# A masked attention layer on one core: the second batch's third value, token sums and a weight's split change places, and seven more clock-keeping products

## The chip, the cores and the metric

The kernel runs on one core of one Trainium2 chip. The metric is device time in microseconds, from one execution of the whole program. The engines of the core work at the same time and meet at semaphores: PE (matrix products, with PEld for its weight loads), DVE (vector work), ACT (exponentials, copies and scalings), POOL (which issues gathers and scatters by index) and SP (which issues the other transfers). The profile gives the granted clock of PE beside the busy times; 1.00 is full speed.

## The reference

Sixteen batches of x, each 512 features by 1024 tokens, go through one attention layer with eight heads of 64, and the result is added to x. Query, key and value are the same projection. The mask (about half of the 1024 tokens of each batch are on) acts on keys and on queries.

```python
xt = jnp.transpose(x, (0, 2, 1))
q = xt @ Wq.T
qh = q.reshape(B, T, NH, dk).transpose(0, 2, 1, 3)
scores = scale * jnp.einsum('bhqd,bhkd->bhqk', qh, qh)
logits = (scores * cmask + (1.0 - cmask) * NEG) * rmask
attn = jax.nn.softmax(logits, axis=-1)
ctx = jnp.einsum('bhqk,bhkd->bhqd', attn, qh)
out = ctx.transpose(0, 2, 1, 3).reshape(B, T, D) @ Wo.T
return x + jnp.transpose(out, (0, 2, 1))
```

A token whose mask is off gets logits of 0 throughout, so its attention is the plain mean of all tokens' q. Such a token needs no scores of its own: all of a batch's tokens that are off share one row, the projection of the mean of x.

## The kernel before

**Tiling.** The batches are worked through in an order of their number of tokens that are on. Of each batch only those tokens are gathered (up to 544, in blocks of 128 and a tail), by `gather` on POOL. `xt` transposes a block of 128 tokens by PE into a buffer `pm` of PSUM (there are two such buffers, shared by all small products), and `xsplit` takes it out as a high half `xh` (float16, by ACT) and a low half `xl` (by DVE). A query block (`query`, 12 products of float16: high with high, high with low, low with high, over four chunks of 128 features) is copied by ACT and masked by DVE. `qsplit` makes high and low halves of a pair of heads on DVE, and four transfers on SP (`xx<-hl`) lay them out for the scores. `value` brings a pair's queries back into rows of tokens by PE: 8 products with `xx` as weights (L687) for every batch but the first. Its squares are summed on DVE; `peaks`, `top` and `bottom` make of them the shift `nm` that the exponentials subtract.

**The mean.** All 1024 tokens of a batch are loaded by SP in four chunks (`load_all`, 512 KB each, two buffers `xm`), and each chunk is summed over its tokens, by ACT (`sum_half`) or, for batch 1, by DVE (`sum_all`, L535). The sums become one or two extra columns of `xh` and `xl`, filled by the last `xt` of the next batch, so the second half of that batch's first query waits for them.

**Stages.** A batch has 18 stages: four pairs of heads, two rounds of scores each, and a few stages between. `scores` is 16 products of PE, followed by four exponentials on ACT which write p. `attend` multiplies p with the values, one stage after the pair's last exponentials; `tail_scores` does the tail of 32 tokens; `recip_sums` and `recip_rows` make the reciprocals of the sums (a transpose by PE at L958, a transfer `rd` to DRAM and two transfers `rb` back, spread over partitions), and `norm` multiplies them in. While batch b is in its scores, the plan of b puts the queries and values of batch b + 1, and the projection of batch b − 1 with the output weight, between them.

**What sets the order.** PE runs in the order in which the program is written: the dictionary `plan` says which small pieces come in which stage, before or after the stage's attend. The other engines' order is made by a scheduler from priorities and its own costs. `behind(i)` adds an edge: what is written under it comes after instruction `i` on the same engine. `free` lists pieces of the other engines by stage; what runs over the end of a batch goes into `owed` and is taken up by the next one. SP, ACT, DVE and POOL take their instructions strictly in the order they were given.

**Start.** Before the first tokens are there, PE computes the places of the tokens and then `warm` products (128x512, float16, whose result nobody reads, L434): 7, then 12, then 1 and 2 between the first transposes. `split` makes the high part of a weight chunk on ACT (L194) and its `rest` the low part on DVE (L197). For the output weight, `wide_high` and `wide_rest` place these: the high parts in stages 9, 10, 16 and 17 of batch 0, the low parts in stages 0 to 3 of batch 1.

The lines that the prediction speaks of: L268 to L272 slots, L394 index, L434 warm, L528 and L535 token sums, L543 loads, L550 mean columns, L553 and L554 x halves, L595 token transposes, L624 and L628 queries and their copies, L658 to L661 the xx transfers, L684 and L687 values, L691 their copy, L738 and L741 peaks, L747 and L757 top and bottom, L760 nm, L773 corr, L798 and L803 tail scores and their exponential, L855 and L879 scores and exponentials, L904 attend, L958 to L971 recip_rows, L1011 norm.

Of the kernel before, what the change touches and what calls it, by code (L numbers as in the profile page):

```python
# [15 lines left out]
ALU = mybir.AluOpType  # L16
# [9 lines left out]
DC = D // P  # L26
# [21 lines left out]
class Fast:  # L48
# [481 lines left out]
    def sum_all(self, b, c, other):  # L530
        s = self.st[b]
        if not other:
            return self.sum_half(b, c)
        with self.behind(self.last_hl), self.nc.allow_low_precision(reason="float32"):
            self.nc.vector.tensor_reduce(s["ms2"][:, c:c + 1], s["xm"][c], AX.X, ALU.add)  # L535

    def load_all(self, b, c, after=None):
# [195 lines left out]
    def peaks(self, b, g):  # L733

        nc, s = self.nc, self.st[b]
        hs = slice(HG * g, HG * g + HG)
        sm = self.smcol[g][:, :HG]
        nc.vector.tensor_reduce(sm.rearrange("p (e h) -> p e h", h=2),  # L738
                                s["sd"][:, 2 * g:2 * g + 2, :].rearrange("p e (k h) -> p e h k", h=2), AX.X, ALU.max)
        if s["A"] > 512:  # L740
            nc.vector.tensor_tensor(sm, sm, s["sdt"][:, hs], ALU.max)  # L741

    def top(self, b, g):

# [403 lines left out]
    def run(self, flag):  # L1148
        B = self.B
        L = lambda f, *a: lambda: f(*a)  # L1150
# [12 lines left out]
        def value(n, e):  # L1163
            return [(0.45, L(self.value, n, e))]
# [11 lines left out]
        for b in range(2, B):  # L1176
            n = 1 if b < B - 3 else 2 if b == B - 3 else 1 if b == B - 2 else len(queue)
# [38 lines left out]
            self.setup2()  # L1216
        for i in range(DC):
            self.load_half(0, i)
        self.warm(12)
        sums0 = [(0, L(self.sum_half, 0, k)) for k in range(2 * DC)]  # L1220
        for _, f in sums0[:4]:
            f()
# [1 line left out]
        with self.tc.high_priority(offset=HPO):  # L1224
            self.slots_of(1)
        self.setup3()
        self.warm(1)
        self.xt(0, 1)
        self.warm(2)
        self.xt(0, 2)  # L1230
        for i in range(DC, 2 * DC):
            self.load_half(0, i, self.pe)
# [49 lines left out]
        todo, carry, owed = [], [], {}  # L1282
        if True:
            for b in range(B + 1):
                o, n = b - 1, b + 1
# [18 lines left out]
                vt = lambda o, g: [(0.25, L(self.value_tail, o, g))] if self.wide[o] > 512 else []  # L1304
                pk, tp, bt = ((lambda o, g, f=f, c=c: [(c, L(f, o, g))]) for f, c in ((self.peaks, 0), (self.top, 0.1), (self.bottom, 0.1)))
                new = [g for g in groups if b == g[0] - 2], [g for g in groups if b == g[0] - 1]
                turn = [(0.1, L(self.recip_rows, b, p)) for p in (1, 2)]
                if n < B:
                    q, x, v = (lambda e, g: query(n, e, g)), xt(n), (lambda e: [(0.25, L(self.value, n, e))])
                    tc, tv = ((lambda g, f=f, c=c: [(c, L(f, n, g))]) for f, c in ((self.tail_copy, 0), (self.value_tail, 0.25)))  # L1310
                    rng = [(0, L(self.range_x, n, c)) for c in range(DC)]
                    ahead = b + 2 < B
                    hot, index = ([(c, L(f, b + 2))] if ahead else [] for f, c in ((self.hot, 0), (self.index, 0.2)))
                    take = [(0, L(self.gather, b + 2, j)) for j in range(5 if self.wide[b + 2] > 512 else 4)] if ahead else []
                    if self.wide[n] == 512:
                        tc = tv = lambda g: []
                    if b:
                        pre = [(0, L(f, *g)) for g in new[0] for f in (self.permute, self.active)]
                        post = [(0.3, L(self.slots, *g)) for g in new[0]]
                        pre += [(0, L(self.facts_sums, *g)) for g in new[1]]  # L1320
                        end = [(0.1, L(self.facts_end, *g)) for g in new[1]]
                        plan = {(0, 0): sums + x[:2], (0, 1): x[2:4],
                                (3, 0): rows + x[4:] + q(0, 0) + second, (3, 1): pre + q(0, 1) + carry, (4, 0): value(b, 3),
                                (5, 1): vt(b, 1) + pk(b, 1),
                                (7, 0): third + q(1, 0) + tp(b, 1), (7, 1): q(1, 1) + post + end + P_(0) + bt(b, 1), (8, 0): tc(0) + v(0) + rng[:2],
                                (10, 0): tv(0) + tail + q(2, 0), (11, 0): hot + rng[2:] + early,
                                (12, 0): turn[:1] + q(2, 1), (12, 1): index + P_(1) + v(1), (13, 0): take[:3],
                                (14, 1): rest + pk(n, 0), (16, 0): turn[1:] + P_(2) + take[3:], (16, 1): q(3, 0) + tp(n, 0) + q(3, 1),
                                (17, 0): bt(n, 0) + v(2) + tc(1) + [(0, L(self.means, n))]}
                        carry = P_(3)  # L1330
                    else:
                        pre = [(0, L(f, *g)) for g in new[0] for f in (self.permute, self.active)]
                        post = [(0.3, L(self.slots, *g)) for g in new[0]]
                        plan = {(0, 0): query(0, 3, 0) + value(0, 2),
                                (3, 0): query(0, 3, 1) + [(0.1, L(self.facts_end, 0, 2))] + x[:1],
                                (5, 0): value(0, 3) + x[1:2] + pk(b, 1), (5, 1): x[2:4],
                                (7, 0): x[4:] + pre + tp(b, 1) + q(0, 0) + bt(b, 1) + q(0, 1), (8, 1): post + q(1, 0),
                                (11, 0): hot + q(1, 1),
                                (12, 0): tc(0) + v(0) + rng[:2] + q(2, 0), (13, 0): index + q(2, 1) + turn[:1],
                                (14, 0): tv(0) + v(1) + rng[2:] + take[:3], (14, 1): pk(n, 0),  # L1340
                                (16, 0): turn[1:] + q(3, 0) + tp(n, 0) + q(3, 1) + take[3:], (16, 1): bt(n, 0),
                                (17, 0): v(2) + tc(1) + [(0, L(self.means, n))]}
                else:

                    places = [("xi", 8), ("xa", 13)]
                    come = [[L(self.late, x, j, *places[k % 2]) for j in range(5, 9)] for k, x in enumerate(rests[b])]
                    leave = [[L(self.rest, x, j) for j in range(5, 9)] for x in rests[b]]
                    free[0] = come[0]
                    for c, l in zip(come[1:] + [[]], leave):
                        free[0] += c + l  # L1350
                    plan = {(0, 0): sums + [(0, L(self.spread, x)) for x in rests[b]], (1, 1): second, (3, 0): rows + carry + value(b, 3) + pk(b, 1),
                            (7, 0): third + tp(b, 1) + P_(0) + bt(b, 1), (11, 0): P_(1), (13, 0): P_(2), (14, 1): [(0, self.ranges)],
                            (16, 1): P_(3)}
                if b in (1, 2):
                    plan[12, 1] += [(0, L(range_w, " oq"[b], c)) for c in range(DC)]
                if b == 0:
                    for c in range(DC):
                        if c > 1:
                            free.setdefault(3 * c + 2, []).append(lambda c=c: self.load("o", c, None, self.beat))
                        free.setdefault((9, 10, 16, 17)[c], []).append(L(wide_high, c))  # L1360
                if b == 0:
                    free.setdefault(3, []).append(L(self.sources, 2, B))
                if b == 1:
                    free.setdefault(1, []).extend(owed.pop(1))
                    for c in range(DC):
                        free.setdefault(c, []).append(L(wide_rest, c))
                if b + 2 < B:
                    if b + 2 not in self.st:
                        self.start(b + 2)
                for k, x in enumerate([x for x in (b + 2, self.extra.get(b + 2)) if x is not None and x < B]):  # L1370
                    if x > b + 2:
                        self.start(x)
                    elif b + 2 in self.extra.values():
                        continue
                    for c in range(DC):
                        at = 3 * c + k + (0 if b else 6)
                        free.setdefault(at, []).append(L(self.load_all, x, c) if b else lambda x=x, c=c: self.load_all(x, c, self.beat))
                        at += 2 if b + 2 in self.extra else 4
                        (free if at < N else owed).setdefault(at % N + (at >= N), []).append(L(self.sum_all, x, c, b == 0 and x == 1))
                def fill(st, half):  # L1380
                    for _, f in plan.get((st, half), []):
# [2 lines left out]
                for st, (p, i) in enumerate(S):  # L1384
# [17 lines left out]
                    if i == 3:  # L1402
                        todo.append(lambda after=None, b=b, p=p: self.attend(b, p, after))
                        if p < 3:
                            free.setdefault(st + 1, []).append(L(self.recip_sums, b, p))
                            if not p or n == B:
                                free.setdefault(st + 2, []).append(L(self.recip_rows, b, p))
                            if p < 2:
                                free.setdefault(min(st + 8 + (b == 0), N - 1), []).append(L(self.norm, b, p))
# [149 lines left out]
```

## Time and profile before

| | |
|---|---|
| median of three runs | 953.54 us (950.12 to 954.99) |
| profiled execution | 952.53 us |
| its span, first to last instruction | 950.8 us |
| mean granted clock of PE | 0.994 |
| PE busy | 930.2 us, 98% of the span |
| DVE, ACT, POOL busy | 720.2, 644.6, 303.8 us |
| PE busy from 0 to 50 us, clock | 41.55 us, 0.97 |
| PE busy from 50 to 100 us, clock | 45.58 us, 0.93 |
| PE busy from 170 to 880 us, clock | 708.41 us, 1.00 |
| PE busy from 880 to 951 us, clock | 64.91 us, 0.99 |

The busy time of an engine is summed over its instructions; matmuls overlap in the pipeline, so the start of one and the start of the next say more of their cost than the length of one. In a row of the timeline the first number is the start in microseconds from the start of the span, the second how long it took; in brackets stands how long the engine sat idle just before, and what ended that. Batch 0 has its scores from about 28 to 73 us, batch 1 from about 77 us on.

### The profile page before, as it was taken

How to read it: one execution, taken by the hardware profiler on the slowest of the kernel's cores; microseconds unless marked ns; L12 is line 12 of the kernel's file. 1: busy time of each engine (PE TensorE's matmuls, PEld its weight loads, DVE VectorE, ACT ScalarE, POOL GpSimd, SP SyncE). 2: the span in 40 equal slices, each digit the busy share in tenths (PEclk: the TensorE clock that was granted, in tenths of full speed). 3: DMA queues.
4: the chain of work that ended last, by engine and by line, in shares of the span. 5: the costliest groups of instructions: out<-in, count | busy, mean ns of one | idle time of the engine just before them, and what ended most of it. 6: DMA issues, size and time to landing. Idle time of an engine off the chain costs nothing. (4 is left out here: it accounts for less than half of the span.)

```text
span 950.8 us, 22847 instructions
## 1 busy us (share of the span) xinstructions
PE 930.2 (98%) x8125; PEld 584.5 (61%) x8125; DVE 720.2 (76%) x2461; ACT 644.6 (68%) x1669; POOL 303.8 (32%) x311
## 2 busy tenths in 40 slices
PE   7998999999999999999999999999999999999997
PEld 4565666666666666666666666666666666565543
DVE  7797787876877767888677788768777788686564
ACT  4786767667676676776767688666767866655651
POOL 2110022151342414325053340623425034353452
PEclk9998999999999999999999999999999999999999
DMA  5776556666575666766567687645767757555552
GB/s 180 203 225 174 160 161 177 179 200 183 167 218 171 189 192 192 214 177 192 170 194 216 200 244 212 189 140 146 223 182 232 224 154 212 146 167 149 182 178 104
DMA packets 78568, 176.30 MB, mean 185 GB/s; under 512 B 14480, under 2 KB 22416, under 8 KB 78448
## 3 DMA queue, kind: packets, MB, share of 16 engines
q1 hardware_dynamic: 57392, 107.09, 40.3%
q0 software_dynamic: 21056, 67.68, 22.5%
q8 instruction: 66, 1.08, 0.5%
q14 instruction: 54, 0.44, 0.1%
HBM read 91.36 MB, written 33.91 MB: 132 GB/s over the span
## 5 line engine op out<-in xcount | busy, mean ns | idle before, releaser
L879 ACT ACTIVATE p<-pss,nm 128x528 f32<-128x528 f32 (+2 forms) x512 | 353.9, 702 | 89.6 <-PE pss L855 88.7
L904 PE MATMUL pss<-p,v 128*64 128x264 f32 (+2 forms) x2048 | 242.6, 390 | 0.0
L855 PE MATMUL pss<-xx 128*128 128x118 f16 (+17 forms) x1856 | 215.1, 289 | 0.4 <-ACT p L879 0.2
L1098 POOL DMA_INDIRECT y_out<-xa,idx x68 | 80.2, 1180 | 409.5 <-DVE nq L762 120.8
L904 PEld LDWEIGHTS pss<-p,v 128*64 128x64 f32 x2048 | 141.5, 137 | 85.9 <-issue 6.5
L855 PEld LDWEIGHTS <-xx 128*128 128x128 f16 (+1 forms) x1856 | 103.3, 97 | 79.8 <-issue 30.2
L624 PE MATMUL pm<-xh,wqh 128*128 128x264 f16 (+5 forms) x512 | 142.1, 278 | 2.3 <-DVE xh L550 0.9
L624 PE MATMUL pm<-xh,wql 128*128 128x264 f16 (+5 forms) x512 | 141.4, 276 | 0.0
L624 PE MATMUL pm<-xl,wqh 128*128 128x264 f16 (+5 forms) x512 | 141.3, 276 | 0.1
L624 PEld LDWEIGHTS <-wqh 128*128 128x128 f16 x1024 | 98.7, 99 | 25.8 <-issue 5.2
L491 POOL DMA_INDIRECT xa<-x_in,idx x68 | 71.6, 1053 | 116.2 <-DMA y_out<-xa,idx 45.7
L879 ACT ACTIVATION_READ_ACCUMULATOR p<-pss,nm 128x1 f32 x512 | 105.3, 206 | 0.0
L1029 PE MATMUL pm<-woh,cl 128*128 128x512 f16 x240 | 90.9, 379 | 0.0
L1029 PE MATMUL pm<-wol,ch 128*128 128x512 f16 x240 | 90.9, 379 | 0.0
L1029 PE MATMUL pm<-woh,ch 128*128 128x512 f16 x240 | 90.9, 379 | 0.0
L628 ACT ACTIVATE q<-pm 128x264 f32<-128x264 f32 (+5 forms) x128 | 50.8, 397 | 45.7 <-PE pm L624 45.7
L691 ACT COPY v<-pm 128x512 f32<-128x512 f32 x62 | 36.4, 586 | 62.0 <-PE pm L687 62.0
L1098 POOL DMA_INDIRECT y_out<-xi,idx x60 | 65.8, 1097 | 32.9 <-PE pss L798 12.4
L1029 PEld LDWEIGHTS <-ch 128*128 128x128 f16 x480 | 46.2, 100 | 44.3 <-issue 0.8
L491 POOL DMA_INDIRECT xi<-x_in,idx x60 | 59.9, 998 | 21.1 <-issue 16.5
L927 ACT COPY c<-pss 128x528 f32<-128x528 f32 (+2 forms) x64 | 38.2, 597 | 39.2 <-PE pss L922 26.6
L716 DVE TENSOR_TENSOR tmp<-pm,par 128x256 f32<-128x256 f32 x26 | 11.0, 423 | 64.8 <-PE pm L713 64.8
(253 smaller groups left out, 1519.6 us busy)
## 6 DMA issues: line engine op xcount, KB each, us to landing
xm<-x_nat_in SPq DMA_DIRECT2D x60, 512.0 KB
xx<-hl SPq DMA_DIRECT2D x208, 136.0 KB
rb<-rd SPq DMA_DIRECT2D x72, 132.0 KB
xx<-hl SPq DMA_DIRECT2D x48, 128.0 KB
pt<-c SPq DMA_DIRECT2D x36, 132.0 KB
pt<-p SPq DMA_DIRECT2D x36, 132.0 KB
rb<-rd SPq DMA_DIRECT2D x32, 136.0 KB
ub<-ud SPq DMA_DIRECT2D x16, 256.0 KB
```

The costliest lines, as they stand in the source:

```text
L491: dma = self.nc.gpsimd.indirect_dma_start(out=tile[:n], out_offset=None, in_=self.x, in_offset=bass.IndirectOffsetOnAxis(ap=idx, axis=0))
L624: self.beat = nc.tensor.matmul(pq, lhsT=w[:, c, e * P:(e + 1) * P], rhs=xx[:, c, cols], start=(k == 0), stop=(k == 3 * DC - 1)).ins
L628: self.copied = nc.scalar.activation(s["q"][:, e, cols], pq, AF.Copy, scale=1.0 / (SX * SW)).ins
L691: nc.scalar.copy(v, pv)
L716: nc.vector.tensor_tensor(split(v), pv.rearrange("p k (h d) -> p k h d", h=2), self.par.unsqueeze(1).unsqueeze(3).broadcast_to([P, 2, 2, D ...
L855: m = nc.tensor.matmul(flat[:, c0:c1], lhsT=w, rhs=x, start=banks[n] not in banks[:n], stop=banks[n] not in banks[n + 1:])
L879: e = nc.scalar.activation(t, flat[:, at:at + A], AF.Exp, bias=s["nm"][p // 2][:, p % 2 * 2 + k:p % 2 * 2 + k + 1], scale=SCALE, accum_out ...
L904: mm = nc.tensor.matmul(pav[k * DK:(k + 1) * DK, g], lhsT=s["v"][p][:, i, k * DK:(k + 1) * DK], rhs=ps[k, i][:, cols], start=(i == 3), sto ...
L927: self.context_out = nc.scalar.copy(c[:, :A].rearrange("p (g c) -> p g c", g=2), pav).ins
L1029: mm = nc.tensor.matmul(po[:cols.stop - cols.start], lhsT=a[:, e, cols], rhs=w[:, e, wide], start=(e == 0 and k == 0), stop=(e == DC - 1 a ...
L1098: dma = self.nc.gpsimd.indirect_dma_start(out=self.out, out_offset=bass.IndirectOffsetOnAxis(ap=idx, axis=0), in_=x, in_offset=None)
```

## The change

- The third value of batch 1 (heads 4 and 5) leaves the end of batch 0's plan, stage 17, and stands in batch 1's stage 4, ahead of the fourth.
- `recip_rows` of batch 0's first pair leaves stage 6, which it had by `free`, for stage 7, behind the last token transposes and the first query of batch 1.
- The token sums of batch 1 on DVE get one more edge each for the last two chunks: the third comes behind the last `peaks` (`self.peak`), the fourth behind the last x half (`self.last_xs`). The last token sum of batch 2 (on ACT) moves from the end of batch 0 to stage 2 of batch 1.
- The output weight's first two high parts move to stages 6 and 7 of batch 0, their low parts to stages 8 and 9 of batch 0, and the last two low parts to stages 4 and 5 of batch 1.
- Loads and token sums of batch 3 come two stages later.
- The clock-keeping products become 17, 2 and 3 instead of 12, 1 and 2.

```diff
@@ sum_all @@
-        with self.behind(self.last_hl), self.nc.allow_low_precision(reason="float32"):
+        with self.behind(self.last_hl, *([self.peak] if c == 2 else [self.last_xs] if c == 3 else [])), self.nc.allow_low_precision(reason="float32"):
             self.nc.vector.tensor_reduce(s["ms2"][:, c:c + 1], s["xm"][c], AX.X, ALU.add)
@@ peaks @@
         if s["A"] > 512:
-            nc.vector.tensor_tensor(sm, sm, s["sdt"][:, hs], ALU.max)
+            self.peak = nc.vector.tensor_tensor(sm, sm, s["sdt"][:, hs], ALU.max).ins
@@ run @@
-        self.warm(12)
+        self.warm(17)
...
-        self.warm(1)
+        self.warm(2)
         self.xt(0, 1)
-        self.warm(2)
+        self.warm(3)
         self.xt(0, 2)
...
-                turn = [(0.1, L(self.recip_rows, b, p)) for p in (1, 2)]
+                turn = [(0.1, L(self.recip_rows, b, p)) for p in range(3)]
...
-                                (12, 0): turn[:1] + q(2, 1), (12, 1): index + P_(1) + v(1), (13, 0): take[:3],
-                                (14, 1): rest + pk(n, 0), (16, 0): turn[1:] + P_(2) + take[3:], (16, 1): q(3, 0) + tp(n, 0) + q(3, 1),
+                                (12, 0): turn[1:2] + q(2, 1), (12, 1): index + P_(1) + v(1), (13, 0): take[:3],
+                                (14, 1): rest + pk(n, 0), (16, 0): turn[2:] + P_(2) + take[3:], (16, 1): q(3, 0) + tp(n, 0) + q(3, 1),
                                 (17, 0): bt(n, 0) + v(2) + tc(1) + [(0, L(self.means, n))]}
+                        if b == 1:
+                            plan[4, 0] = value(b, 2) + plan[4, 0]
...
-                                (7, 0): x[4:] + pre + tp(b, 1) + q(0, 0) + bt(b, 1) + q(0, 1), (8, 1): post + q(1, 0),
+                                (7, 0): x[4:] + pre + tp(b, 1) + q(0, 0) + bt(b, 1) + q(0, 1) + turn[:1], (8, 1): post + q(1, 0),
...
-                                (16, 0): turn[1:] + q(3, 0) + tp(n, 0) + q(3, 1) + take[3:], (16, 1): bt(n, 0),
-                                (17, 0): v(2) + tc(1) + [(0, L(self.means, n))]}
+                                (16, 0): turn[2:] + q(3, 0) + tp(n, 0) + q(3, 1) + take[3:], (16, 1): bt(n, 0),
+                                (17, 0): tc(1) + [(0, L(self.means, n))]}
...
-                        free.setdefault((9, 10, 16, 17)[c], []).append(L(wide_high, c))
+                        free.setdefault((6, 7, 16, 17)[c], []).append(L(wide_high, c))
+                        if c < 2:
+                            free.setdefault(8 + c, []).append(L(wide_rest, c))
...
                 if b == 1:
-                    free.setdefault(1, []).extend(owed.pop(1))
-                    for c in range(DC):
-                        free.setdefault(c, []).append(L(wide_rest, c))
+                    for k in (1, 2):
+                        free.setdefault(k, []).extend(owed.pop(k))
+                    for c in (2, 3):
+                        free.setdefault(c + 2, []).append(L(wide_rest, c))
...
-                        at = 3 * c + k + (0 if b else 6)
+                        at = 3 * c + k + (0 if b > 1 else 2 if b else 6)
...
-                        at += 2 if b + 2 in self.extra else 4
+                        at += 2 if b + 2 in self.extra and (b or k or c < DC - 1) else 4
...
-                            if not p or n == B:
+                            if n == B or b and not p:
                                 free.setdefault(st + 2, []).append(L(self.recip_rows, b, p))
```

## The prediction

> **What bounds the kernel now.** I read the page first: it says which engine is full.
>
> ```profile
> span 950.8 us, 22847 instructions
> PE 930.2 (98%) x8125; PEld 584.5 (61%) x8125; DVE 720.2 (76%) x2461; ACT 644.6 (68%) x1669; POOL 303.8 (32%) x311
> ```
>
> PE is the bound. An engine that is 98% busy can gain in two ways only: from its few idle microseconds, and from stretches in which it is busy at a lower clock. So the table of windows comes next: PE is busy 708.41 of the 710 us from 170 to 880, and 50 us from 120 to 170 lack 0.28. Nothing is to be had there; the last 71 us lack 6.1, but the change touches nothing in them. What it can move lies before 120 us, where PE lacks 8.5 us in 0 to 50 and 4.4 in 50 to 100, at clocks of 0.97 and 0.93. The windows of 1 and 2 us show where (columns: span, PE, PEld, DVE, ACT, POOL busy, clock, DMA share, GB/s).
>
> ```profile
> 11.00:12.00 1.00, 0.17 (x1) 0.00 (x0) 1.00 (x7) 0.75 (x3) 0.69 (x2) 1.00 0.93 270
> 12.00:13.00 1.00, 0.00 (x0) 0.00 (x0) 0.77 (x4) 0.58 (x2) 0.84 (x1) 1.00 0.71 180
> 14.00:15.00 1.00, 1.00 (x8) 0.60 (x6) 0.96 (x5) 0.47 (x2) 0.10 (x1) 0.83 0.63 213
> 15.00:16.00 1.00, 0.99 (x4) 0.37 (x3) 0.97 (x4) 0.44 (x1) 0.00 (x0) 0.50 0.78 246
> 18.00:19.00 1.00, 1.00 (x11) 0.92 (x9) 0.96 (x8) 0.19 (x1) 0.00 (x0) 0.97 0.84 248
> ...
> 74.00:76.00 2.00, 0.00 (x0) 0.00 (x0) 1.34 (x6) 1.32 (x3) 1.24 (x2) 1.00 1.00 245
> 76.00:78.00 2.00, 0.95 (x10) 0.63 (x11) 1.60 (x9) 0.17 (x1) 0.65 (x1) 0.52 0.94 303
> 78.00:80.00 2.00, 2.00 (x13) 0.97 (x13) 1.14 (x5) 0.83 (x3) 0.00 (x0) 0.50 0.55 212
> 82.00:84.00 2.00, 2.00 (x15) 1.21 (x15) 1.41 (x3) 1.74 (x5) 0.00 (x0) 0.77 0.69 169
> ```
>
> The reader is to see two pairs: PE stands still, and a little later its clock is halved. From the shares, half clock lasts from 14.66 (0.34 of that us) to 18.06, 3.40 us, and from 76.08 to 82.92, 6.84 us, twice as long. Half of that is lost: 1.7 and 3.4 us. The timeline of PE and its waits name what it stood still for:
>
> ```profile
> PE pm L687 <- DMA xx<-hl: 3.2, 2, 2.5
> PE pss L595 <- DMA xa<-x_in,idx: 1.9, 1, 1.9
> ...
> 44.66 0.33 PE L958 MATMUL pm<-ident,rcol 128*128 128x128 f32 x1 [0.98 <-DVE xl L554]
> 76.30 0.21 PE L687 MATMUL pm<-two,xx 128*128 128x64 f16 x1 [2.49 <-DMA xx<-hl]
> 77.26 0.53 PE L687 MATMUL pm<-two,xx 128*128 128x64 f16 x7 [0.75 <-DMA xx<-hl]
> 92.80 0.29 PE L624 MATMUL pm<-xh,wqh 128*128 128x274 f16 x1 [0.94 <-DVE xh L550]
> ```
>
> Idle gaps of 0.94 and 0.98 us kept the clock; 1.87 (11.17 to 13.04) and 3.24 did not. So the third value of batch 1 costs 3.24 of waiting and 3.4 of clock, and the wait for the first gathered tokens, which no order of PE removes, costs 1.7 of clock behind it.
>
> **The change, part by part.** Durations are rows of this execution; the sum is made against its own 952.53 us (span 950.8, 1.7 around it). The median of the runs shown is 953.54.
>
> *Seven more clock-keeping products.* At full clock one costs 0.215 us (twelve in the 2.75 us from 8.42). Five end at 12.25 instead of 11.17, under the wait for the gather (13.04), so they cost nothing and the gap shrinks from 1.87 to 0.8, below the gaps that kept the clock. The other two lie on PE: xt(0,1) moves from 14.14 to 14.36, xt(0,2) from 15.66 to about 15.5, because the three products ahead of it run at full clock. The first query needs the second block's low half (DVE, 15.47 + 0.69 = 16.16), so it starts at 16.2 instead of 16.54, and takes 1.3 us (the same twelve products from 18.61 on at full clock, with the transposes out) instead of 2.07: 17.5 against 18.61. The fourth gather is issued at 13.15 and the first took 3.9, so it is there at 17.05. DVE keeps up, because the built program puts two more query-weight low parts (0.37 each) into DVE's 1.11 us wait before 13.88: its fourth x half comes 1.1 earlier too. Gain 1.1; bounds: 1.7 (all of the lost clock) and a loss of 0.43 (the two products, nothing kept).
>
> *Row sums of pair 0 (recip_rows) moved behind two queries of batch 1.* At 44.66 the transpose waited 0.98 for a pm buffer. Now the scores behind it (44.83) start at 43.7, since their exponentials ended at 41.5. What is late next: pm has two buffers and the moved transpose takes one between the queries, so q(1,1,0) waits for ACT's copy of q(1,0,1), behind a 1.07 sum (49.37): it starts about 0.3 earlier, not 1.1. Its queue matters too: rd and two rb issues now stand directly ahead of the four xx issues of pair 0 on SP, and rb waits for rd, 2.5 us from 45.42 to 47.91. xx then issues about 0.6 later; PE asks for it at 59.6, the trace's packets of this size end at about 57.5, and a 512-KB load is gone from ahead of pair 1's. Gain 0.3; bounds 1.0 and a loss of 0.6. On the facts' product (0.28 wait on DVE eh) DVE's order puts eh ahead of a 0.69 square: gain 0.2.
>
> *Output weight.* Two high parts on ACT (0.52 pitch) move into ACT's 1.23 wait before 42.71: nothing, covered by that wait. Two low parts (0.6 each) enter DVE at 53, where it is full to 72; but the third token sum (1.13 pitch) leaves the same stretch, behind the peaks. The next PE step that needs DVE there, the transpose of the peaks, has 0.7 of slack (71.31 to 72.02). Nothing, bounds 0.3 either way.
>
> *Third value to batch 1's stage 4.* PE ends `bottom` at 73.67, and the exponentials of the last scores ended at 73.19, so the first scores of batch 1 run at 73.7 to 75.4, not 77.60 to 80.64. Both pm buffers are free (copies at 73.5 and, since a 1.07 sum leaves ACT's place between them, 74.3), the first three gathers have landed: transposes to 76.4, attend (3.7) to 80.1. POOL's order is the same: the fourth and fifth gathers are issued at 74.46 and 75.71, and with the first one's 3.9 they are there at 78.4 and 79.6, ahead of their transposes at 81. What is late next is ACT:
>
> ```profile
> 74.72 0.69 DVE L1011 TENSOR_TENSOR c<-c,rb 128x512 f32<-128x512 f32 x1 [0.66 <-DMA rb<-rd]
> 75.33 0.15 DVE L760 TENSOR_SCALAR nm<-pss 128x4 f32<-128x4 f32 x1
> ```
>
> DVE takes the shift nm behind a product that waits for rb. rb is issued 0.5 later now (two xx issues ahead, not one). So nm at about 75.9, corr at 77, and ACT: exponential, two x halves, three exponentials (0.7, 0.5 each) end at 81.2, then the moved token sum (1.2), then the tail's exponential (0.7) to 83.1. The second scores need that one: 83.2 against 87.87. The chain behind it on DVE to the mean columns (L550) was 4.8 us after the tail's exponential; the four weight parts leave it, the last token sum stays in it: about 4.9. So q(2,0,1) starts at 88.1 against 92.80. Gain 4.7, with PE idle about 1.1 and 1.35 on the way. Bounds: 6.6 (both waits and all clock back) and 0 (the wait returns in another place).
>
> *What batch 1 pays later.* Value 2 and 3 now come in a row: value 3 needs the buffer of q(2,0,1), copied 0.4 after it, about 0.2 of wait; and DVE gets two squares (1.3) and two weight parts (1.3) more ahead of peaks(1,1), whose slack was 1.2 (102.92 to 104.15); it also waited 0.5 there. About 0.4. Loads and sums of batch 3 two stages later: they are needed a batch on, nothing. Loss 0.6; bounds 0 and 1.8.
>
> Sum: −1.1 − 0.3 − 0.2 − 4.7 + 0.6 = −5.7; 952.5 − 5.7 = **946.8 us**. Past 120 us nothing differs.
>
> **The rivals.**
> 1. *The extra products keep nothing.* For it: the clock could follow something else than the gap. Against: both drops follow the two longest gaps. Then the 1.1 goes and the two products stay on PE: 948.3. The Trainium skill, "TensorE: Matmul & The Clock Gate", section Part 1, drops the clock after an idle window of about 3.4 us; read strictly, 1.87 would drop nothing and five products would be useless. This trace does not agree: the clock fell behind 1.87. The page's free-running window agrees with drop lengths of 3.40 and 6.84.
> 2. *The clock still halves once in batch 1.* The two waits I leave (1.1 near 82, 1.35 near 87) are longer than those which kept the clock. One stretch of 3.4 at half: 946.8 + 1.7 = 948.5.
> 3. *The wait moves to the second scores (other side).* rb lands late, since DMA is 0.94 to 1.00 busy there; nm, and all exponentials of batch 1, follow it one for one. From about 2.3 us of lateness the gap is 3.4, the clock halves twice as before (3.4), and 946.8 + 2.3 + 3.4 = 952.5 equals before: later than that is slower. At 3.5 late: 953.7; at 8, 958.2. For it: rb took from 69.1 to 74.7; against: the loads ahead of it are as many as before.
>
> **How the numbers follow.** Forecast 0.56 (own range 945 to 948.8), rival 1 0.15, rival 2 0.15, rival 3 0.14, of which 0.05 beyond 8 us late. A measurement tells about 0.5% from no change: 948.8 and 958.3. Under 948.8: 0.50 of the forecast, 0.08 and 0.07 of rivals 1 and 2: 0.65; over 958.3: 0.05; between: 0.30. The range 944.5 to 951.5 goes from the bound of 6.6 for the third value to rival 3 at its mild end, and leaves 0.15 out above and a little below.
>
> **What would show it.** In the profile after: no half clock at 14 to 18 and none at 76 to 83; no L687 wait in PE's list; first scores of batch 1 straight behind `bottom`; new PE waits of 1 to 1.5 us on ACT's tail exponential and on xh L550; the transposes of batch 1's later peaks up to 0.5 late; from 120 us on the same busy PE. I am wrong if the scores of batch 1 wait for nm or if the clock drops behind the new gaps.

## The result and the profile after

Set against the kernel before, twelve executions each: 949.16 us after (948.13 to 950.81), 953.01 us before (949.72 to 954.99). The ratio is 0.9968, 95% interval 0.9955 to 0.9981: faster by 3.85 us in the medians and 3.0 in the means, where 946.8 would have been 6.7 under the 953.54 shown before (and 5.7 under the profiled execution, against which the sum was made). A second comparison (experiment 4) gave 947.31 against 951.07, ratio 0.9970 [0.9957, 0.9983], 3.8 in the medians and 3.0 in the means. So the direction holds, with 3 to 4 us, and the size forecast does not. The profiled execution of after took 949.01 us, with a span of 947.2.

The first lines of the page of after, and below them its list of PE's waits (line, what it waited for, us in total, times, longest):

```profile
span 947.2 us, 22862 instructions
PE 927.7 (98%) x8132; PEld 583.7 (62%) x8132; DVE 720.0 (76%) x2461; ACT 644.5 (68%) x1669; POOL 304.4 (32%) x311
```

```profile
PE pm L208 <- DVE quad L169: 3.9, 1, 3.9
...
PE pss L904 <- DVE nm L760: 1.0, 1, 1.0
PE pm L624 <- DVE xh L550: 0.9, 1, 0.9
PE pss L595 <- DMA xa<-x_in,idx: 0.8, 2, 0.6
PE pss L855 <- ACT p L803: 0.8, 1, 0.8
...
PE pss L375 <- DVE m L750: 0.5, 1, 0.5
...
PE pss L798 <- ACT p L879: 0.4, 1, 0.4
...
PE pm L687 <- DMA pt<-p: 0.3, 1, 0.3
```

PE is as full as before. The 3.2 on `xx` are gone from the list, and the wait for the first gathered tokens has shrunk from 1.9 to 0.8. In their place stand 1.0 on nm, 0.8 and 0.4 on exponentials, 0.5 on the peaks, 0.3 in front of a value: waits that before did not have in these places. (The first row is an accident of the start: DVE's first step, L205, took 1.10 us in this execution and 0.23 in that of before, and PE began 0.94 later; in the profile of after in experiment 4 it began at 2.90.)

The windows that answer to those shown of before (span, PE, PEld, DVE, ACT, POOL, clock, DMA share, GB/s):

```profile
13.00:14.00 1.00, 0.37 (x3) 0.21 (x3) 1.00 (x5) 0.47 (x2) 0.79 (x1) 1.00 0.80 201
15.00:16.00 1.00, 1.00 (x8) 0.68 (x7) 0.96 (x5) 0.20 (x2) 0.21 (x1) 1.00 0.58 213
18.00:19.00 1.00, 1.00 (x11) 0.94 (x10) 1.00 (x4) 0.34 (x1) 0.00 (x0) 1.00 0.33 106
74.00:76.00 2.00, 1.72 (x17) 1.12 (x15) 0.11 (x1) 0.00 (x0) 1.60 (x2) 1.00 0.89 221
76.00:78.00 2.00, 1.29 (x12) 0.92 (x14) 2.00 (x9) 0.93 (x3) 0.00 (x0) 1.00 1.00 379
82.00:84.00 2.00, 1.24 (x13) 0.74 (x11) 0.75 (x4) 2.00 (x7) 0.00 (x0) 1.00 0.82 187
```

The clock stays at 1.00 in both places where it was 0.50 to 0.52 before. PE still stands still in the second place, but in pieces: 0.28 of the two us from 74, 0.71 of the next two, 0.76 from 82. The timeline names the pieces:

```profile
75.89 0.69 DVE L1011 TENSOR_TENSOR c<-c,rb 128x512 f32<-128x512 f32 x1 [2.51 <-DMA rb<-rd]
76.50 0.15 DVE L760 TENSOR_SCALAR nm<-pss 128x4 f32<-128x4 f32 x1
76.71 3.67 PE L904 MATMUL pss<-p,v 128*64 128x256 f32 x32 [1.00 <-DVE nm L760]
80.80 0.65 PE L798 MATMUL pss<-xx 128*32 128x272 f16 x16 [0.41 <-ACT p L879]
88.37 0.29 PE L624 MATMUL pm<-xh,wqh 128*128 128x274 f16 x1 [0.94 <-DVE xh L550]
90.70 0.47 PE L687 MATMUL pm<-two,xx 128*128 128x64 f16 x8 [0.25 <-DMA pt<-p]
102.60 0.16 PE L375 MATMUL pss<-eh,on 128*128 128x2 f16 x1 [0.48 <-DVE m L750]
```

DVE stood 2.51 us in `norm`, waiting for rb, with the shift nm behind it. nm reads a buffer `pss`, and PE's attend, which writes one, waited 1.0 for it. With 0.76 ahead of the second scores and 0.17 ahead of a query, the new waits add up to 1.0 + 0.41 + 0.76 + 0.17 + 0.25 + 0.48 = 3.07 us, where 3.24 were removed. In this execution the idle time of PE was thus moved and cut up, and what was won was clock.

Step by step along PE, starts in us before and after, and the gain counted from PE's first product (3.00 and 3.94), which takes the accident of the start out:

| step | before | after | gain | forecast by then |
|---|---|---|---|---|
| first scores of batch 0 | 27.94 | 27.66 | 1.22 | 1.1 |
| its last scores | 68.96 | 68.28 | 1.62 | 1.6 |
| second scores of batch 1 | 87.87 | 83.23 | 5.58 | 6.3 |
| q(2,0,1) of batch 2's tokens | 92.80 | 88.37 | 5.37 | |
| next scores | 94.72 | 91.01 | 4.65 | |
| facts' product, L375 | 105.66 | 102.60 | 4.00 | |
| a transpose, L958 | 118.53 | 115.46 | 4.01 | 5.7 |

### The profile page after: what moved, and what is told of

It is laid out like the page before. It is cut to its first block, busy times and chain, and to the rows that moved or that the text cites. A ratio compares the mean times of both kernels' runs of the same rounds, so it can differ in the third digit from the quotient of the medians.

```text
span 947.2 us, 22862 instructions
## 1 busy us (share of the span) xinstructions
PE 927.7 (98%) x8132; PEld 583.7 (62%) x8132; DVE 720.0 (76%) x2461; ACT 644.5 (68%) x1669; POOL 304.4 (32%) x311
## 5 line engine op out<-in xcount | busy, mean ns | idle before, releaser
L927 ACT COPY c<-pss 128x528 f32<-128x528 f32 (+2 forms) x64 | 38.3, 598 | 37.1 <-PE pss L922 25.6
```

Source lines behind the costliest of these rows:

```text
L927: self.context_out = nc.scalar.copy(c[:, :A].rearrange("p (g c) -> p g c", g=2), pav).ins
```

## The experiments

Theory A throughout: the kernel gained by two things, the clock behind the two gaps and the wait of the third value, and part of that wait came back behind rb and nm. The rivals differ from set to set, and each expectation spells its own out. Each set of four ran on one chip, with the kernel before among them. "Clock loss" below is (1 − mean granted clock) × span of an execution, averaged over a kernel's executions; it is the most that the clock can have cost PE, since half clock costs nothing while PE waits. Part of it costs nothing at all: in all 18 profiles the clock is also halved in the last 0.4 to 4.2 us of the span, in which PE has no instruction left, and that makes 0.2 to 2.1 us of the loss. In after's profile this is all of it (a mean clock of 0.98 over these 67 us, the third number from the end, is 2.7 us at half clock, a loss of about 1.4; from 944.33 on PE has nothing to do):

```profile
880.00:947.00 67.00, 61.16 (x409) 31.21 (x406) 36.07 (x105) 30.08 (x83) 29.04 (x28) 0.98 0.43 145
```

**1. One part alone, one part undone.** The third value's new place alone:

```diff
+ if b == 1:
+     plan[4, 0] = value(b, 2) + plan[4, 0]
...
- (17, 0): v(2) + tc(1) + [(0, L(self.means, n))]}
+ (17, 0): tc(1) + [(0, L(self.means, n))]}
```

> The kernel before with one edit: the third value of batch 1 moves to its stage 4. Theory A (the wait of 3.2 us and the half clock of 3.4 us behind it were the bulk, and what comes back is small): faster by 3 to 4 us, 949 to 950, no half clock between 70 and 95 us. Theory B (most of the change's gain is the start, kept by the seven products; the wait of the value only moves to the shift nm and the tail's exponential): within 1 us of before, 952 to 954. Theory C (the value's move pays only together with the moved token sums and weight parts): 952 to 954 as well, with DVE late before the mean columns.

The clock-keeping products alone:

```diff
- self.warm(12)
+ self.warm(17)
...
- self.warm(1)
+ self.warm(2)
  self.xt(0, 1)
- self.warm(2)
+ self.warm(3)
```

> The kernel before with 17, 2 and 3 clock-keeping products instead of 12, 1 and 2. Theory A: 1.2 us faster, 951.8, full clock from 14 to 18 us, and the wait and the half clock near 76 to 83 us as before. Theory B: 3 us faster, 950. If the products keep nothing: 953 to 953.5, half clock at 14 to 18 us.

The changed kernel with the old products (12, 1, 2), and the changed kernel with the value in its old place:

> The changed kernel with 12, 1 and 2 clock-keeping products. Theory A: 1.2 us slower than the changed kernel, 950.4, half clock for 3.4 us near 15. Theory B: 952 to 953.

> The changed kernel with the third value back at the end of batch 0. Theory A: 952 to 953, with a wait on the transfer xx of 2 to 3 us and a half clock behind it. Theory B: 949.5 to 950.5.

| kernel | median us | ratio to before, 95% | mean clock loss us |
|---|---|---|---|
| before (35 executions, the others 12 each) | 952.46 | | 3.18 |
| value alone | 949.71 | 0.9967 [0.9950, 0.9985] | 1.50 |
| products alone | 951.23 | 0.9988 [0.9975, 1.0001] | 2.69 |
| after, old products | 950.19 | 0.9972 [0.9958, 0.9985] | 1.11 |
| after, old value | 951.67 | 0.9995 [0.9979, 1.0011] | 2.46 |

The times came close to what theory A said: the value's place carries the change, 2.7 us alone, and without it 0.8 is left, by an interval that includes no change (951.67, where 952 to 953 were expected). The products alone gained 1.2, by an interval from 2.4 to just past nothing. One expectation missed in the profile. With the old products the long gap was to halve the clock again; in the profiled execution it did not. The wait for the first gathered tokens, timeline of PE, in "after, old products" and in "value alone" the waits' row for the same gap:

```profile
13.41 0.63 PE L595 MATMUL pss<-ident,xa 128*128 128x128 f32 x4 [0.91 <-DMA xa<-x_in,idx]
```

```profile
PE pss L595 <- DMA xa<-x_in,idx: 1.9, 1, 1.9
```

In the first the gap was short by itself. In the second it is as long as in before, 1.9 us, and the granted clock of that whole execution was 1.0. So the same gap costs the clock in one execution and not in another.

The stretch from 76 to 83 us is steadier. Here it is in "products alone" and in "after, old value", which have the value in its old place:

```profile
76.00:83.00 7.00, 6.12 (x47) 3.86 (x49) 4.88 (x19) 3.83 (x10) 0.88 (x1) 0.76 0.91 272
76.00:83.00 7.00, 6.76 (x53) 4.43 (x55) 5.32 (x19) 4.54 (x12) 0.87 (x1) 0.76 0.67 228
```

A mean clock of 0.76 is half clock for about half of the stretch, 3.41 us, where before had it for 6.83, nearly all of it. The "others alone" of experiment 4 have 0.76 as well. So the drop behind this gap came in all four of these profiles, but only before's had it at double length; none of the nine profiles with the moved value has it (the disturbed set of experiment 4 left out).

**2. The clock alone.** In the kernel before, the wait of the third value is filled with products, so that PE waits as long but not idly:

```diff
+ def fill_gap(self, n):
+     t = self.pm([P, 4, P])
+     for _ in range(n):
+         self.nc.tensor.matmul(t, lhsT=self.on16, rhs=..., start=True, stop=True)
...
- (17, 0): v(2) + tc(1) + [(0, L(self.means, n))]}
+ (17, 0): [(0, L(self.fill_gap, 11))] + v(2) + tc(1) + [(0, L(self.means, n))]}
```

> The kernel before with eleven more products (128x512, 0.215 us each, 2.4 us) ahead of the third value, at its old place: the wait for the transfer stays, PE only looks busy in it. Theory A (most of the change's gain is the clock behind that wait, the waits themselves came back in smaller pieces): no half clock between 70 and 95 us, 1.5 to 2.5 us faster than before, with the mean clock loss about 1.5 us instead of the 3.2 of the 35 runs before. Theory B (the gain is the wait itself): within 0.7 us of before, a little slower if the products delay the value.

Measured beside before at 952.26: 951.08, ratio 0.9992 [0.9977, 1.0006]; mean 951.12 against 952.15, between what the two theories expected. The remaining wait in its timeline of PE (its line numbers are five higher), and the clock of the stretch:

```profile
77.14 0.36 PE L692 MATMUL pm<-two,xx 128*128 128x64 f16 x7 [0.62 <-DMA xx<-hl]
```

```profile
76.00:83.00 7.00, 6.38 (x63) 4.09 (x62) 7.00 (x23) 5.03 (x13) 0.92 (x1) 1.00 0.72 219
```

The clock loss fell from 2.97 to 1.50, as far as it fell when the value was moved, and the time by 1.0 in the mean (by its interval, from 2.2 down to a loss of 0.6). The moved value alone brought the clock loss down to the same 1.50 and gained 2.4 in the mean (952.59 to 950.22). So the clock behind this gap, which the prediction priced at 3.4, is worth about 1 us over many executions, and 2.2 at most. That the other 1.4 of the moved value is waiting is likely but not shown: the two gains come from different sets, and their intervals overlap. The products themselves may cost a little where `xx` comes before they are done: time less clock loss rose by 0.4 (949.18 to 949.61), which is within the scatter.

**3. The wait that came back.** The changed kernel, with `norm` of pair 1 of batch 0 put behind `top` of the next batch on DVE, so that nm is free of rb:

```diff
+ def norm_behind(b, p):
+     with self.behind(self.st[b + 1]["top"]):
+         self.norm(b, p)
...
- ...append(L(self.norm, b, p))
+ ...append(L(norm_behind if b == 0 and p == 1 else self.norm, b, p))
```

> The changed kernel with one more edge: the norm of pair 1 of batch 0 comes behind the shift nm of batch 1 on DVE, so nm no longer waits for rb. Theory A (the waits of 1.0, 0.4 and 0.8 us at batch 1's attend, tail and second scores are the removed wait in another place, and rb is their cause): all three go, second scores at about 81 instead of 83.2, 1.5 to 2.2 us faster than the changed kernel, 947 to 947.6. Theory B (ACT is the cause, its order of halves, exponentials and the moved token sum): attend starts at once but the tail and the second scores wait longer, less than 0.7 us faster.

Before with the moved value and the products, without the other edits:

> The kernel before with the value's move and the seven products, without the moved row sums, token sums, weight parts and loads. Theory A (these other edits are worth nothing or cost a little): 949 or less, as fast as the changed kernel or up to 1 us faster. Theory C (they are needed): 950 to 951.

Shift first, and besides, value(1,2) behind the query of stage 3 and the last token sum of batch 1 (`sum_all(1,3)`) in stage 0:

> The changed kernel with the shift first as in the run with that name, the last token sum of batch 1 on DVE ahead of the tail's exponential instead of behind it, and the third value in the wait for the mean columns (stage 3, behind the first half of batch 2's first query). Theory A: no wait of more than 0.5 us is left on PE between 75 and 105 us, 2.5 to 3.5 us faster than the changed kernel, 946 to 946.7. If another wait takes their place (the fourth gather at the transposes, or ACT's copies in front of the exponentials): 947 to 948.

Shift first took 946.97 (six executions), ratio 0.9949 [0.9931, 0.9968]. Its timeline of DVE shows the order turned round, and no wait for rb:

```profile
72.48 0.15 DVE L760 TENSOR_SCALAR nm<-pss 128x4 f32<-128x4 f32 x1
74.81 0.69 DVE L1011 TENSOR_TENSOR c<-c,rb 128x512 f32<-128x512 f32 x1
```

The 1.0, 0.4 and 0.8 of after are gone from its list of PE's waits; the 0.9 on xh L550 and the 0.5 on m L750 stay. Against the first comparison's 949.16 that is the 2.2 us of those three rows, but from different sets (see 4).

Value and products took 950.54 [0.9969, 0.9997], where theory A had 949 or less and theory C 950 to 951: it seems to need some help of the other edits, though after itself is not in this set. The row that they take away is this one in its timeline, against 0.94 in after:

```profile
87.80 0.28 PE L624 MATMUL pm<-xh,wqh 128*128 128x274 f16 x1 [1.95 <-DVE xl L554]
```

Closing two more gaps showed no gain over shift first: 948.05 (eight executions) [0.9938, 0.9971], where theory A had 946 to 946.7, and 947 to 948 if another wait took their place. One did (timeline of PE):

```profile
94.99 0.30 PE L958 MATMUL pm<-ident,rcol 128*128 128x128 f32 x1 [1.29 <-DVE rcol L951]
```

**4. Side by side.** The other edits alone; shift first and the changed kernel on one chip; and before with the moved value and the shift first only.

> The other edits of the change alone (row sums of pair 0, output weight parts, token sums, peak order, loads and sums of batch 3), with the old place of the third value and 12, 1 and 2 clock-keeping products. Theory A (the change lives by the clock behind two gaps and by the value's wait; the rest is worth what its rows say, 0.3 for the row sums and 0.2 for the facts' product): 951.7, that is 0.5 under a kernel before of about 952.2. Theory B (the rest carries more than a microsecond by itself): 951.0 or less. Theory C (the rest pays only once the third value has moved): 952.2 or more.

> The changed kernel with the shift nm of batch 1 taken ahead of the normalisation that waits for rb, beside the changed kernel itself on the same chip. Theory A (the wait for nm behind rb is where part of the removed wait came back, 1.0 directly and 0.4 and 0.8 behind it): 947.2, 2.0 under the changed kernel. Rival (the earlier figure came from the chip or the moment): within 0.7 of the changed kernel.

> The changed kernel as it is, as the measure for the run with the shift first. Theory A: 949.3, about 3 under the kernel before. If the time depends on the chip by more than that: anything from 948 to 951 with the shift-first kernel following it.

> The kernel before with two edits only: the third value of batch 1 in its stage 4, and the shift nm ahead of the normalisation that waits for rb. Theory A (the wait behind rb is a cost of the moved value, whatever the other edits): the moved value alone took 949.7 with waits of 0.8 on nm and 0.4 and 0.4 behind it; with them gone 948.1, and the wait for the first gathered tokens stays as it was. Theory B (the other edits are what lets the shift pay): 949.3 or more.

This set tells little. On its chip every kernel took some 30 us more, before 984.24, with single executions of one kernel 12 us and more apart: others alone 979.52 [0.9924, 0.9989], shift first 977.10 [0.9896, 0.9970], after 983.36 [0.9946, 1.0017], value and shift first 981.90 [0.9953, 1.0030]. The costliest groups show what was different: the row of ACT's copy L927 in after, first in the first profile, then in this set (busy, mean ns of one, idle before it):

```profile
L927 ACT COPY c<-pss 128x528 f32<-128x528 f32 (+2 forms) x64 | 38.3, 598 | 37.1 <-PE pss L922 25.6 <-PE pss L904 11.5
```

```profile
L927 ACT COPY c<-pss 128x528 f32<-128x528 f32 (+2 forms) x64 | 38.3, 598 | 61.1 <-remote 22.5 <-PE pss L922 16.7 <-PE pss L904 7.9
```

The copy itself is as long to the nanosecond; ACT stood before it for 24 us more, put down to something outside the core's own engines. PE stood still too, and it also ran more often at half clock: the mean clock loss is 7 to 9 us in these four kernels. What the cause was the runs don't show. So the four went again, on a chip without it.

> The other edits alone, as before, on a chip without the stalls. Theory A: 0.5 under the kernel before. Theory B: 1.2 or more under it. Theory C (they pay only beside the moved value): level with it or above.

> The changed kernel with the shift ahead of the normalisation. Theory A (part of the removed wait came back behind rb): 2.0 under the changed kernel of this set. Rival (the chip made the earlier figure): within 0.7 of it.

> The changed kernel as it is, the measure for the others of this set: 3 under the kernel before, with a mean clock loss of 1.1 to 1.5 against 3.

> The kernel before with the moved value and the shift first only. Theory A: about 4 under the kernel before and 1.5 under what the moved value alone gave against it (2.8). Theory B (the other edits are what lets the shift pay): no further under the kernel before than 3.

| kernel | median us | mean us | ratio to before, 95% | mean clock loss us |
|---|---|---|---|---|
| before (34 executions, shift first 11, the others 12) | 951.07 | 951.02 | | 2.68 |
| others alone | 949.78 | 949.97 | 0.9986 [0.9971, 1.0002] | 2.14 |
| value and shift first | 948.95 | 949.01 | 0.9981 [0.9965, 0.9996] | 1.66 |
| after | 947.31 | 948.02 | 0.9970 [0.9957, 0.9983] | 1.26 |
| shift first | 947.03 | 947.28 | 0.9959 [0.9945, 0.9973] | 1.20 |

After came as expected, 3.0 under before in the means. The other edits alone gained 1.0 in the means, between theory A's 0.5 and theory B's 1.2. Two expectations of theory A fell here. Shift first is only 0.3 under after in the median and 0.7 in the mean (the interval of that difference, redrawn from the executions, is −1.8 to +0.3), not 2.0. And value with shift first is 2.0 under before, not 4: no better than the value alone had been. The timeline of after in this set suggests why the first fell (DVE, and PE's next wait):

```profile
73.85 0.69 DVE L1011 TENSOR_TENSOR c<-c,rb 128x512 f32<-128x512 f32 x1 [0.93 <-DMA rb<-rd]
74.46 0.16 DVE L760 TENSOR_SCALAR nm<-pss 128x4 f32<-128x4 f32 x1
81.19 1.78 PE L855 MATMUL pss<-xx 128*128 128x472 f16 x16 [0.74 <-ACT p L803]
```

rb was waited for 0.93 us here and 2.51 in the first profile; PE had no wait for nm at all. How late rb lands differs from execution to execution (0.93, 1.49 and 2.51 in three profiles of the changed kernel and its old-products form), so the wait that the first profile shows is not a fixed cost of the change. Of the five profiles on undisturbed chips with the moved value and nm still behind rb, PE waited for nm in two, after (1.00) and "value alone" (0.81), and these are the two in which L205 took 1.10 us; whether the late start causes it was not tested. For the second, value with shift first waits elsewhere in its profile, in the place that the other edits relieve (timeline of PE):

```profile
83.78 0.43 PE L595 MATMUL pm<-ident,xt 32*128 32x32 f32 x4 [0.89 <-DVE xl L554]
85.02 0.28 PE L624 MATMUL pm<-xh,wqh 128*128 128x272 f16 x1 [0.80 <-DVE xl L554]
```

So the other edits are probably worth something: about a microsecond alone in the means, by an interval that reaches just past no change, and 1.7 us [0.7, 2.7] between "value and shift first" and "shift first", where the products are in the difference too.

## Why the prediction was wrong in its size

Right were the direction, the place (all before 120 us) and, in the profile, the mechanism and most rows. The first seven products and the edits up to the end of batch 0 gave 1.62 in the profile, where 1.6 was forecast; no half clock at 14 to 18 or at 76 to 83; the first scores of batch 1 straight behind `bottom` (72.99 behind 72.85); waits near 83 and 88 (0.76 and 0.94) where it put 1.1 and 1.35. That the second scores start at 83.23, where the sum said 83.2, is luck: the sum's 83.2 counts neither the 1.6 gained ahead of it nor the late start of 0.94. With both it is 82.5, so these scores came 0.7 late.

**The step that failed is the clock in "Third value to batch 1's stage 4 ... Gain 4.7" and in "Gain 1.1" of the products.** The prediction said: "Half of that is lost: 1.7 and 3.4 us", read that off one execution, and took 3.4 and 1.1 of it, 4.5 us, as a gain against every execution. Against that one execution the term held: after's profile has no half clock before its last 3 us, where PE is done, and the 4.0 us won there instead of 5.7 fell short by waits (below). Against the others it did not. The profiled execution of before had a mean clock of 0.994. Of 94 executions of that kernel on the three undisturbed chips six were that low or lower. In the last set before lost 2.68 us of clock on average (± 0.24, standard error), and after 1.26 (± 0.21), which in both undisturbed profiles of after is all at the end, where PE has nothing to do. The difference is 1.4 us, by its interval (redrawn from the executions) 0.8 to 2.0: less than half of 4.5. Among before's executions there, a microsecond of clock loss goes with 0.83 us of time, so the clock was worth (2.68 − 1.26) × 0.83 = 1.2 us, not 4.5. Compared at the same clock, the eight executions of before at 0.999 took 948.9 on average, the seven of after at 0.999 947.7: 1.2 us less, which is what the forecast had left without its clock, 5.7 − 4.5 = 1.2. That match may be luck, since executions that keep their clock may have had shorter waits too; in the set of experiment 1 the same comparison gives the moved value alone no gain (949.7 on four executions of before, 949.8 on five). With the clock at its average size the sum would have been 1.2 + 1.2 = 2.4; measured in that set were 3.0 in the means and 3.8 in the medians.

**The wait was also read off one execution.** 3.24 us on `xx` in before's profile; 1.05 in "products alone", 2.1 in "after, old value" and 3.14 in "others alone", where the value stands in the old place too (the first has 1.52 on a copy ahead of it). That gap halved the clock for 6.83 us in before's profile and for 3.41 in these three.

**What batch 1 pays later** was 0.6, and in the profile it is 1.57 (5.58 at the second scores, 4.01 at the end). One thing had been left out of that sum: the moved value's own products, which now come later (with their wait of 0.25, 0.72 of the gain was gone by the next scores). The other is larger than forecast: "peaks(1,1)" was to be late by 0.4, and 0.65 of the gain went there. The last step of the peaks (L741) starts at 100.01 instead of 102.77, which counted from PE's first product is 3.70 earlier, where PE had gained 4.65. The transpose did not wait for it, but L375 waited 0.48 for m, which stands behind `norm` and the halves after it on DVE, as it did before.

**Rival 3 came in part.** "I am wrong if the scores of batch 1 wait for nm": in the first profile the attend in front of them did, for 1.0, because nm came at 76.50. The sum had 75.9, which with the 1.6 gained ahead of it and the late start of 0.94 is 75.2, and no one waiting for it. So nm was 1.3 late, and the second scores 0.7. In the profile of after in experiment 4 PE did not wait for it. As a rival it was priced from 2.3 us of lateness on; what came was little more than half of that, and it halved no clock.

**Rival 1 is not settled, rival 2 did not come.** The profiles suggest that the products keep the clock: on the undisturbed chips none of the eight with the new products had half clock from 14 to 18 us, and two of the six with the old ones did. Over all executions it is little: about 0.5 us of clock loss alone (3.18 to 2.69, by an interval that includes nothing), and the changed kernel with the old products lost no more (1.11) than after (1.26). The clock did not fall behind the new waits of batch 1 in any of the nine profiles with the moved value. The Trainium skill, "TensorE: Matmul & The Clock Gate", section Part 1, says that the window in which the chip looks for idleness runs freely, so that the moment of a change depends on the phase at which the kernel meets it. The runs here fit that: behind a gap of 1.9 us the clock fell in one execution and held in another.

**Where a gap lies decides.** The traces also show how a gap costs the clock. In each of them the changes of the clock lie a whole number of 3.413 us apart, on a grid whose place against the kernel differs from execution to execution. In before the gap of 1.87 us falls almost wholly into one stretch of that grid, 11.24 to 14.66, in which PE is busy for 1.62 of 3.41 us, and the next stretch is at half clock. In "value alone" a grid line at 13.38 splits the same gap: PE is busy for 2.44 us of the stretch ahead of it and for 2.21 of the one behind, and the clock holds. From 10 to 935 us, on the undisturbed chips, all six stretches at full clock with less than half of their time busy (0.25 to 0.47 of it) were followed by half clock, and none with 0.51 or more was; on the disturbed chip two with 0.44 and 0.46 were not, so no sharp limit is shown. In before the stretch from 76.09, already at half clock and busy for 2.46 of 3.41 us, was followed by a second one at half clock, so its drop is 6.83 long.

The prediction used that page of the Trainium skill for the lengths of the drops, which are 3.41 or 6.83 us in the traces, and did not draw from it that whether a gap costs the clock can differ between executions of one kernel.

What stays open: how much of the moved value's gain is clock and how much waiting, and how the rest of the gain splits between the products, the row sums and the weight parts. The intervals of "products alone" and "others alone" include no change, and the parts alone add up in the means to 2.4 + 1.0 + 1.0 = 4.4, more than the 3.0 of the whole. That would follow if the same lost clock can be saved only once, but the scatter of the means allows a plain sum too.

## What to carry to other kernels

Price a drop of the clock by how often it happens, not by one trace: list the granted clock of all executions first, and take their mean against the profiled one's. A wait on a transfer that differs from one execution to the next by 2 us belongs in the range and not in the sum. When work is moved out of a gap, write its own time on the far side of the sum too, and ask what now stands in front of the next engine's queue; after one long gap was cut into waits of a microsecond or less, the profile showed no half clock there even though PE stood still about as long as before.

## What the runs showed of the hardware

- The same gap on PE, 1.9 us, led to half clock in the profile of before and to none in that of "value alone"; one of 2.26 in "others alone" led to it, one of 1.95 in "value and products" did not. All stretches of half clock ahead of the one at the end were 3.41 us long or twice that.
- DVE's first step L205 took 0.23 us in one execution of after and 1.10 in another, which shifts PE's start by about 0.9 us; of all 18 profiles four have 1.10 or more.
- The median of the same kernel was 951.07, 952.26, 952.46 and 953.01 in four sets, and 984.24 on one chip, where ACT's copies were as long as elsewhere (598 ns) and the engines stood still between their instructions, and where the profile of after has a mean clock of 0.990.
- The kernel with the shift first was the fastest of all (946.97 and 947.03 in two sets, 0.9949 and 0.9959 of before); its lead over the changed kernel, 0.7 us in the mean on one chip, is within what these runs can tell from nothing.
